# Listing each expert's first three pages first, in a two-layer graph and mixture-of-experts kernel

## The chip, the core and the metric

The kernel runs on one core of a Trainium2 chip. The metric is the device time of one execution in microseconds (us); lower is better. The engines have these names in the profile: PE is the matrix engine (its weight loads are PEld), DVE the vector engine, ACT the scalar engine, POOL the general engine, which here issues the indirect DMAs, and SP the engine whose queue issues most of the other DMAs. A suffix q (SPq, ACTq) marks what an engine's queue issues.

## What is computed

The input is 128 graphs of 64 nodes with 256 features, so 8192 tokens of 256 numbers, all in f32. There are two layers, and each is a graph convolution followed by a mixture of experts:

```
x = x + gnn0(ln(x), adj)        # adj @ h, 256->1024, rms norm, silu, 1024->256
x = x + ffn0(ln(x))             # 64 experts, the best 6 per token: sum_k score_k * (x @ lattice[e_k]), 256x256 each,
                                #   then out_w, a residual and a layer norm
x = x + gnn1(ln(x), adj)        # adj @ h @ W_rel + h @ W_root, relu
x = x + ffn1(ln(x))             # 8 experts, the best 2 per token: relu(x @ W1[e] + b1) @ W2[e] + b2, 256->512->256
```

Which experts a token goes to depends on the data. Worked out with the reference's arithmetic on its inputs, the 64 experts of ffn0 get between 278 and 1654 tokens each, 49152 in all; of the first 1024 tokens an expert gets between 45 and 201.

## The kernel before, in words

The work is done in 32 blocks of 256 tokens and in four stages, one after the other.

**Stage 1 (L550 to L760)** computes gnn0 block by block, chooses six experts per token and sends each token's row six times into a table in device memory, `r0x`, by indirect DMAs from POOL (`send`, L304, 12 a block). Each expert has chunks of rows of its own in that table. A row carries its token, the number of its place in the answer (column D) and its weight (column D+1). At the end `page_table` (L326) lists on DVE the **pages** that are to be worked off: a page is 128 rows of one expert. The order of the list is: all the full pages, expert by expert, and then the partial page of each expert. The list is made with a running sum over `num`, which holds the number of full pages of 64 experts and then 0 or 1 for their partial pages (V = 128 columns); `kind` counts how many entries of the running sum lie at or below a page's number.

**Stage 2 (L763 to L815)** works off the pages in pairs. `fetch` (L770) loads a page into `px` on SP's queue, 12 pairs ahead, into 16 buffers for each half of a pair; `flip` (L780) turns it on PE into `pxT`; `apply` (L790) multiplies it by its expert's matrix in `lat` (64 matrices, 131072 bytes a partition, resident), DVE scales the product into `py_s` (8 buffers, L806), and POOL scatters the 128 rows to their places in `r0y` (`answer` in the code) by one indirect DMA (`reply`, L311). 212 pairs (424 pages) are always done; 12 pairs more lie in a branch (`tc.If`, L814) that is taken when the list is longer than 424 pages. Any routing fits in 447 pages.

**Stage 3 (L819 to L1028), the fused pass**, does for each block: load the six answers of each of its tokens (`load3`, L848: `y<-r0y`, two DMAs a block, then `xn1` and `x1`), sum them by PE (`mixture`, L859), `out_proj`, the residual and layer norm (`layer_out_h`, `_a`, `_b`, `_c`), all of gnn1, the choice of two experts and the sending of rows into `r1x`. The pass is staggered: the list in L1007 names for each step which stage of which block comes next, and PE, DVE and ACT take their instructions in just that order (`manual_schedule`, L462). `y` has two buffers. Before the pass the second router `r1` is made (L820): constants on POOL and DVE, and two DMAs of zeros from a `filler` tile (L141 and L183 on SP's queue). Ten small loads of weights and rows come from ACT's queue (L830 to L839), and DVE adds the two gate rows (L840) before anything else of the pass.

A DMA of `y` reads `r0y`, which all replies write; so each of them waits until every reply before it in the program, those of the branch included, is done or skipped.

**Stage 4 (L1031 to L1106)** does ffn1 in pages of 256 rows, in the same manner with the router `r1`; its answers are added into the output by DMAs (L319). Its first three pages, one each of the experts 0 to 2, are known early (`look`, L146) and are listed apart.

The pools of on-chip memory are laid one behind the other: the constants, then `lat`, then stage 2's pool `wx0`, which starts with the `px` buffers. When stage 2 is over, the pools of stages 3 and 4 (`keep`, `wx1`, `c3`, `work3`) are laid from the start of `lat` on, over `lat` and part of `wx0`. A tile that lies on old memory waits for those that last used it.

Of the kernel before, what the change touches and what calls it, by code (L numbers as in the profile page):

```python
# [9 lines left out]
F32 = mybir.dt.float32  # L10
BF16 = mybir.dt.bfloat16
# [5 lines left out]
ALU = mybir.AluOpType  # L17
AX = mybir.AxisListType
PSUM = bass.MemoryType.PSUM
P = 128  # L20
# [7 lines left out]
class Ops:  # L28


    def __init__(self, nc, small, ident, eps):
        self.nc, self.small, self.ident, self.eps = nc, small, ident, eps
# [46 lines left out]
class Router:  # L79
# [12 lines left out]

    def __init__(self, tc, pool, small, dram, n, D, E, K, T, pg, S, epoch, name, total=None):
        nc = tc.nc
        self.tc, self.nc, self.pool, self.small = tc, nc, pool, small
        self.n, self.D, self.E, self.K, self.T, self.pg, self.S, self.name = n, D, E, K, T, pg, S, name
# [8 lines left out]
        self.W = D + 2  # L107
        assert T == 2 and epoch == 4 and n % self.EP == 0 and S % pg == 0 and (5 * T * P <= S or S >= n)
        assert self.pages <= 4 * P and self.spare + pg < 2 ** 24
        self.tri = pool.tile([P, P], BF16, name=name + "tri")  # L110
        self.ones = pool.tile([P, P], BF16, name=name + "ones")
        make_upper_triangular(nc, self.tri, diag=False)
        nc.gpsimd.memset(self.ones, 1.0)
        self.expert = self.iota([P, 2 * E], [[1, 2 * E]], 0, "expert")
        self.page = self.iota([P, 4], [[1, 4]], 4, "page")
        self.total, self.each = total, (1 if total is not None else K)
        self.dest = self.iota([P, T, K], [[P * self.each, T], [0 if self.each == 1 else 1, K]], self.each, "dest")
        self.base = pool.tile([P, E], F32, name=name + "base")
        nc.vector.tensor_scalar(self.base, self.expert[:, :E], float(self.pitch), None, op0=ALU.mult)
        self.zero = pool.tile([P, 2 * E], F32, name=name + "zero")  # L120
        nc.gpsimd.memset(self.zero, 0.0)
        self.map = pool.tile([P, self.J, E], F32, name=name + "map")
        nc.gpsimd.memset(self.map, 0.0)
# [22 lines left out]
    def look(self, m):  # L146
# [11 lines left out]
        v.tensor_scalar(self.firsts[:, :m], t, float(self.spare), None, op0=ALU.add)  # L158
        self.full_pages -= m

    def iota(self, shape, pattern, m, name):
        t = self.pool.tile(shape, F32, name=self.name + name)
        i = self.small.tile([P, 384], I32, name="iota", bufs=1)[:, :t.free_size()]
        if len(shape) == 3:
            i = i.rearrange("p (a b) -> p a b", b=shape[2])
        self.nc.gpsimd.iota(i, pattern=pattern, base=0, channel_multiplier=m)
        self.nc.vector.tensor_copy(t, i)
        return t
# [19 lines left out]
    def choose(self, logits):  # L188

        nc, T, E, K, n = self.nc, self.T, self.E, self.K, self.name  # L190
        top = self.small.tile([P, T, 8], F32, name=n + "top")
        idx = self.small.tile([P, T, 8], U32, name=n + "idx")
        for t in range(T):
            nc.vector.max(top[:, t, :], logits[:, t, :])
            nc.vector.max_index(idx[:, t, :], top[:, t, :], logits[:, t, :])
        which = self.small.tile([P, T, K], F32, name=n + "which")
        nc.vector.tensor_copy(which, idx[:, :, :K])
        hot = self.work.tile([P, T, K, E], BF16, name=n + "hot")
        nc.vector.tensor_tensor(hot, self.expert[:, :E].unsqueeze(1).unsqueeze(1).to_broadcast([P, T, K, E]),
                                which.unsqueeze(3).to_broadcast([P, T, K, E]), op=ALU.is_equal)  # L200
        return top, hot

# [103 lines left out]
                    in_=xs[:, t, k, :], in_offset=None)  # L306
                self.alone(i.ins, *groups)

    def reply(self, x, y):

        i = self.nc.gpsimd.indirect_dma_start(  # L311
            out=self.answer[:, :],
            out_offset=bass.IndirectOffsetOnAxis(ap=x[:, self.D:self.D + 1].bitcast(I32), axis=0),
            in_=y, in_offset=None, bounds_check=self.n * self.K - 1, oob_is_err=False)
        self.alone(i.ins, "reply")

    def add(self, i, x, y):

# [7 lines left out]
    def page_table(self, scratch):  # L326

        nc, v, E, J, n, pg = self.nc, self.nc.vector, self.E, self.J, self.name, self.pg
        V = 2 * E
        used = [0]  # L330

        def small(shape, _):
# [9 lines left out]
        if J > 1:  # L342
            t = small([E], "t")
# [2 lines left out]
            v.tensor_add(self.last, run, t)  # L346
        else:
            v.tensor_copy(self.last, run)
        num, cum = small([V], "num"), small([V], "pcum")
        full, part = num[:, :E], num[:, E:]  # L350

        v.tensor_scalar(full, cnt, 1.0 / pg, (pg - 1.0) / (2 * pg), op0=ALU.mult, op1=ALU.subtract)
        v.tensor_scalar(full, full, MAGIC, None, op0=ALU.add)
# [3 lines left out]
        if self.taken is not None:  # L357
            assert J == 1
            v.tensor_sub(full, full, self.taken)
            v.scalar_tensor_tensor(self.map[:, 0, :], self.taken, float(pg), self.map[:, 0, :],  # L360
                                   op0=ALU.mult, op1=ALU.add)
        v.tensor_tensor_scan(cum, num, self.zero, 0.0, op0=ALU.add, op1=ALU.add)
        self.total_pages = self.pool.tile([P, 1], I32, name=n + "total")
        v.tensor_copy(self.total_pages, cum[:, V - 1:V])
        le, at, ate = small([4, V], "le"), small([4, V], "pat"), small([4, E], "pate")
        kind, ispart, exp, nth, row, no = (small([4], x) for x in ("pkind", "ppart", "pexp", "pnth", "prow", "pno"))
        start = small([J, 4], "pstart")
        self.tab = self.pool.tile([P, 2, 4], I32, name=n + "tab")
        v.tensor_tensor(le, wide(cum, 1, V), wide(self.page, 2, V), op=ALU.is_le)
        v.tensor_reduce(kind, le, op=ALU.add, axis=AX.X)  # L370
        v.tensor_tensor(at, wide(self.expert, 1, V), wide(kind, 2, V), op=ALU.is_equal)
        v.tensor_mul(le, le, wide(num, 1, V))
        v.tensor_reduce(nth, le, op=ALU.add, axis=AX.X)
        v.tensor_sub(nth, self.page, nth)
        v.tensor_add(ate, at[:, :, :E], at[:, :, E:])
        v.tensor_mul(le[:, :, :E], at[:, :, E:], wide(full, 1, E))
        v.tensor_reduce(no, le[:, :, :E], op=ALU.add, axis=AX.X)
        v.tensor_add(nth, nth, no)
        for j in range(J):
            v.tensor_mul(le[:, :, :E], ate, wide(self.map[:, j, :], 1, E))  # L380
# [7 lines left out]
        v.tensor_scalar(row, row, float(self.spare), None, op0=ALU.subtract)  # L388
        v.tensor_mul(row, row, no)
        v.tensor_scalar(self.tab[:, 0, :], row, float(self.spare), None, op0=ALU.add)  # L390
        v.tensor_scalar(ispart, kind, float(E), None, op0=ALU.is_ge)
        v.scalar_tensor_tensor(exp, ispart, -float(E), kind, op0=ALU.mult, op1=ALU.add)
        v.tensor_scalar(self.tab[:, 1, :], exp, float(E - 1), None, op0=ALU.min)

    def fill_end(self, e):
# [49 lines left out]
def two_layer_gnn_moe_kernel(ctx: ExitStack, tc: tile.TileContext, a: dict, out: bass.AP):  # L445
# [7 lines left out]
    T = 2  # L453
# [4 lines left out]
    KH = H0 // P  # L458
    K0 = 6
    E1, F1, _ = a["L1_ffn_W2"].shape  # L460
    KF = F1 // P
    ctx.enter_context(tc.manual_schedule(engines={ENG.PE, ENG.DVE, ENG.Activation}))  # L462

# [60 lines left out]

    x1_dram = [dram.tile([C, D], F32, name=f"x1_{b}") for b in range(NB)]
    xn1_dram = [dram.tile([C, D], F32, name=f"xn1_{b}") for b in range(NB)]
    r0 = Router(tc, const, small, dram, N, D, E0, K0, T, P, 14 * P, 4, "r0")
    W = r0.W

    lat_pool = tc.tile_pool(name="lat", bufs=1)  # L530
    lat = lat_pool.__enter__().tile([P, E0, KD, D], F32, name="lat")
# [18 lines left out]
    with tc.tile_pool(name="c0", bufs=1) as c0, \  # L550
# [161 lines left out]
        def place(b):  # L712
            B = blocks[b]
            r0.normalize(*B["w"], B["xs"])
            r0.send(r0.places(b, B["hot"]), B["xs"])

        def load_lattice(b):
            n = free[0] // 16
# [44 lines left out]
    with tc.tile_pool(name="wx0", bufs=3) as wx, \  # L763
# [6 lines left out]
        def fetch(j):  # L770
            Q = pairs[j]
            for q in range(2):
                i = 2 * j + q
                if i % 4 == 0:
                    regs["row"] = r0.load(0, i, ENG.SP)
                if i < r0.pages:
                    Q["px", q] = px = wx.tile([P, 1, W], F32, name=f"px{q}", bufs=16)
                    r0.fetch(i, regs["row"][i % 4], px)

        def flip(j):  # L780
# [9 lines left out]
        def apply(j):  # L790
            Q = pairs[j]
            if j < E0:
                r0.fill_end(j)
            if j % 2 == 0:
                regs["e"] = r0.load(1, 2 * j, ENG.PE)
            py = py_pool.tile([P, 2, D], F32, name="py")
            y = wx.tile([P, 2, D], F32, name="py_s", bufs=8)
            n = min(2, r0.pages - 2 * j)
            for q in range(n):
                for k in range(KD):  # L800
                    nc.tensor.matmul(py[:, q, :], lhsT=Q["xT"][:, k, ts(q, P)],  # L801
                                     rhs=lat[:, ds(regs["e"][(2 * j + q) % 4], 1), k, :].rearrange("p o d -> p (o d)"),
                                     start=(k == 0), stop=(k == KD - 1))
            for q in range(n):
                px = Q["px", q]
                nc.vector.tensor_scalar(y[:, q, :], py[:, q, :], px[:, 0, D + 1:D + 2], None, op0=ALU.mult)  # L806
                r0.reply(px[:, 0, :], y[:, q, :])


        stages = ((-12, fetch), (0, apply),  # L810
                  (-2, lambda j: flip(j) if j < 4 else None), (-3, lambda j: flip(j) if j >= 4 else None))
        likely = (r0.likely_pages + 3) // 4 * 2
        staggered(likely, stages)
        with tc.If(r0.needed(2 * likely)):  # L814
            staggered(npair, stages, likely)  # L815
    lat_pool.__exit__(None, None, None)


    keep = ctx.enter_context(tc.tile_pool(name="keep", bufs=1))  # L819
    r1 = Router(tc, keep, small, dram, N, D, E1, 2, T, 2 * P, N, 4, "r1", total=out)  # L820
    fw1 = a["L1_ffn_W1b1"]
    F1W = fw1.shape[2]
    fw2 = keep.tile([P, E1, KF, D], F32, name="fw2")
# [1 line left out]
    with tc.tile_pool(name="c3", bufs=1) as c3, \  # L825
# [13 lines left out]
        gbias = load_rows(c3, "L1_ffn_bias")  # L839
        nc.vector.tensor_add(bg, bg, gbias)  # L840
        one = c3.tile([P, P], F32, name="one")
        nc.gpsimd.memset(one, 1.0)
        blocks = [dict() for _ in range(NB)]
        pg = pmix.tile([P, T, E1], F32, name="pg")
        FIRST = 3
# [2 lines left out]
        def load3(b):  # L848
            B = blocks[b]
            B["y"] = y = work.tile([P, T, K0, D], F32, name="y")  # L850
            for t in range(T):
                nc.sync.dma_start(out=y[:, t], in_=r0.answer[ts(b * T + t, P * K0), :].rearrange("(p k) d -> p k d", k=K0))
            B["xn1"] = xn1 = work.tile([P, T, D], F32, name="xn1", bufs=3)
            nc.sync.dma_start(out=xn1, in_=by_tile(xn1_dram[b]))
            B["x1"] = x1 = work.tile([P, T, D], F32, name="x1", bufs=3)
# [283 lines left out]
```

## Time and profile before

| | us |
|---|---|
| median of five runs (2135.41 to 2142.46) | 2138.4 |
| the profiled execution, its own time | 2138.43 |
| its span, first to last instruction | 2136.7 |
| busy in the span: PE / DVE / ACT / POOL | 1938.2 / 1187.1 / 1019.6 / 1166.4 |
| 424 replies (L311) on POOL: busy, mean of one | 412.5, 0.973 |
| 424 scalings (L806) on DVE: mean of one | 0.479 |
| first and last reply issued | 669.82 and 1210.30 |
| last product of stage 2 ends on PE | 1185.09 |
| first `y` load issued on SP's queue | 1214.57 |
| first sum of the fused pass on PE | 1220.67 |
| one block of the fused pass in its steady part | 11.3 |

Times in the trace count from the start of the span; the time of the execution is 1.7 us longer than its span. A line of the timeline gives start, length, engine, line, operation and how many were merged; in brackets is how long the engine sat idle before it and what ended that. A line of the waits gives the total, how often, and the longest. A line of the windows gives, for one stretch, the length, then the busy time and number of instructions of PE, PEld, DVE, ACT and POOL, the clock granted to PE (1.00 is full), the busy share of the DMA engines and what they moved in GB/s.

### The profile page before, as it was taken

How to read it: one execution, taken by the hardware profiler on the slowest of the kernel's cores; microseconds unless marked ns; L12 is line 12 of the kernel's file. 1: busy time of each engine (PE TensorE's matmuls, PEld its weight loads, DVE VectorE, ACT ScalarE, POOL GpSimd, SP SyncE). 2: the span in 40 equal slices, each digit the busy share in tenths (PEclk: the TensorE clock that was granted, in tenths of full speed). 3: DMA queues.
4: the chain of work that ended last, by engine and by line, in shares of the span. 5: the costliest groups of instructions: out<-in, count | busy, mean ns of one | idle time of the engine just before them, and what ended most of it. 6: DMA issues, size and time to landing. Idle time of an engine off the chain costs nothing. (4 is left out here: it accounts for less than half of the span.)

```text
span 2136.7 us, 37321 instructions
## 1 busy us (share of the span) xinstructions
PE 1938.2 (91%) x10564; PEld 1683.3 (79%) x10564; DVE 1187.1 (56%) x3958; ACT 1019.6 (48%) x2037; POOL 1166.4 (55%) x1146
## 2 busy tenths in 40 slices
PE   7999999999945989998888289999988999999997
PEld 6888888888835778877777278888877888888886
DVE  5889989899882333333333168888883222222221
ACT  5888788888831222222222056666653333333332
POOL 0376666666675777777777503333343344444444
PEclk9999999999967999999999699999998999999998
DMA  3244455553377887666665379888735766666665
GB/s 109 96 138 150 145 163 165 165 165 131 123 238 230 273 257 239 209 207 208 208 204 160 109 282 331 294 262 273 266 116 129 183 157 165 163 162 164 162 160 109
DMA packets 284094, 398.96 MB, mean 187 GB/s; under 512 B 56536, under 2 KB 237928, under 8 KB 283888
## 3 DMA queue, kind: packets, MB, share of 16 engines
q1 hardware_dynamic: 204032, 247.67, 39.4%
q0 software_dynamic: 64800, 136.14, 21.4%
q10 hardware_dynamic: 15056, 12.69, 1.8%
q8 instruction: 94, 1.54, 0.3%
q14 instruction: 112, 0.92, 0.2%
HBM read 223.89 MB, written 177.69 MB: 188 GB/s over the span
## 5 line engine op out<-in xcount | busy, mean ns | idle before, releaser
L304 POOL DMA_INDIRECT r0x<-xs,r0row x384 | 396.0, 1031 | 256.0 <-issue 171.7
L311 POOL DMA_INDIRECT r0y<-py_s,px x424 | 412.5, 973 | 140.8 <-DMA r0y<-py_s,px 55.2
L801 PE MATMUL py<-lat,pxT 128*128 x1696 | 410.4, 385 | 40.4 <-DVE py_s L806 22.8
L806 DVE TENSOR_SCALAR py_s<-py,px 128x256 f32<-128x256 f32 x424 | 185.7, 479 | 361.8 <-PE py L801 185.8
L801 PEld LDWEIGHTS py<-lat,pxT 128*128 128x128 f32 x1696 | 307.2, 191 | 90.5 <-ACT pxT L788 30.7
L319 POOL DMA_INDIRECT out_x<-py_s,px x138 | 214.5, 1554 | 298.7 <-DMA out_x<-py_s,px 208.9
L788 ACT COPY pxT<-pt 128x512 f32<-128x512 f32 x212 | 124.1, 586 | 429.2 <-PE pt L786 300.6
L1077 ACT ACTIVATE phid<-ph,pw 128x256 f32<-128x256 f32 x276 | 130.9, 474 | 323.1 <-issue 170.6
L1075 PE MATMUL ph<-pxT,pw 128*128 128x256 f32 x1104 | 251.5, 381 | 0.7 <-ACT pxT L1066 0.7
L1095 PE MATMUL py<-fw,phid 128*128 (+1 forms) x1104 | 249.7, 379 | 0.0
L630 PE MATMUL ph<-lat 128*128 128x256 f32 x1024 | 232.9, 386 | 11.0 <-DVE lat L652 10.4
L663 PE MATMUL ps<-lat 128*128 128x256 f32 x1024 | 237.7, 381 | 0.0
L1075 PEld LDWEIGHTS ph<-pxT,pw 128*128 128x128 f32 x1104 | 211.0, 191 | 30.1 <-ACT pxT L1066 1.1
L630 PEld LDWEIGHTS ph<-lat 128*128 128x128 f32 x1024 | 195.2, 193 | 39.4 <-DVE lat L652 10.0
L1095 PEld LDWEIGHTS py<-fw,phid 128*128 128x128 f32 x1104 | 204.5, 190 | 25.0
L663 PEld LDWEIGHTS ps<-lat 128*128 128x128 f32 x1024 | 193.2, 191 | 24.7
L304 POOL DMA_INDIRECT r1x<-xs,r1row x128 | 130.2, 1017 | 116.8 <-ACT xn3T L978 63.2
L786 PE MATMUL pt<-ident,px 128*128 128x128 f32 x848 | 128.3, 275 | 35.8 <-DMA px<-r0x 35.8
L786 PEld LDWEIGHTS pt<-ident,px 128*128 128x128 f32 x848 | 106.6, 142 | 57.7 <-issue 36.3
L1089 DVE TENSOR_SCALAR p<-p 128x2 f32<-128x2 f32 x69 | 12.0, 174 | 226.3 <-ACT p L1088 226.3
L1098 DVE TENSOR_TENSOR py_s<-py,pb 128x512 f32<-128x512 f32 x69 | 47.8, 692 | 156.0 <-PE py L1095 151.2
L866 PE MATMUL ps<-ident,y 128*128 128x128 f32 x768 | 93.7, 280 | 38.4 <-DMA r1x<-r1filler 35.6
(271 smaller groups left out, 2876.7 us busy)
## 6 DMA issues: line engine op xcount, KB each, us to landing
px<-r0x SPq DMA_DIRECT2D x424, 129.0 KB
y<-r0y SPq DMA_DIRECT2D x64, 768.0 KB
pw<-in_L_ffn_W1b SPq DMA_DIRECT2D x69, 514.0 KB
px<-r1x SPq DMA_DIRECT2D x69, 258.0 KB
x<-x SPq DMA_DIRECT2D x64, 256.0 KB
pb<-in_L_ffn_b SPq DMA_DIRECT2D x69, 128.0 KB
r0x<-r0filler ACTq DMA_DIRECT2D x64, 129.0 KB
lat<-in_x SPq DMA_DIRECT2D x32, 256.0 KB
```

What stands on the lines that cost most here:

```text
L304: i = self.nc.gpsimd.indirect_dma_start(out=self.table[:, :], out_offset=bass.IndirectOffsetOnAxis(ap=row[:, t, k:k + 1], axis=0), in_=xs[ ...
L311: i = self.nc.gpsimd.indirect_dma_start(out=self.answer[:, :], out_offset=bass.IndirectOffsetOnAxis(ap=x[:, self.D:self.D + 1].bitcast(I32 ...
L319: i, d = f"{self.name}add{i}", self.nc.gpsimd.indirect_dma_start(out=self.total[:, :], out_offset=bass.IndirectOffsetOnAxis(ap=x[:, self.D ...
L630: nc.tensor.matmul(ph[:, c, :], lhsT=w1[:, k, ts(2 * j + c, P)], rhs=B["aggT"][:, k, :], start=(k == 0), stop=(k == KD - 1))
L663: nc.tensor.matmul(B["po"][:, t, :], lhsT=B["hT"][:, c, ts(t, P)], rhs=w2[:, c, :], start=False, stop=(t == T - 1 and c == KH - 1))
L786: nc.tensor.transpose(pt[:, k, ts(q, P)], Q["px", q][:, 0, ts(k, P)], ident)
L788: nc.scalar.copy(xT[:, :, :n * P], pt[:, :, :n * P])
L801: nc.tensor.matmul(py[:, q, :], lhsT=Q["xT"][:, k, ts(q, P)], rhs=lat[:, ds(regs["e"][(2 * j + q) % 4], 1), k, :].rearrange("p o d -> p (o ...
L806: nc.vector.tensor_scalar(y[:, q, :], py[:, q, :], px[:, 0, D + 1:D + 2], None, op0=ALU.mult)
L1075: nc.tensor.matmul(ph, lhsT=w[:, k * F1 + c * P:k * F1 + (c + 1) * P], rhs=Q["xT"][:, k, :], start=(k == 0), stop=(k == KD - 1))
L1077: nc.scalar.activation(hid[:, c, :], ph, AF.Relu, bias=w[:, KD * F1 + c:KD * F1 + c + 1], scale=1.0)
L1095: nc.tensor.matmul(py[:, t, :], lhsT=Q["hid"][:, c, ts(t, P)], rhs=fw2[:, ds(e, 1), c, :].rearrange("p o d -> p (o d)"), start=(c == 0), s ...
```

## The change

1. `page_table` now lists three kinds of pages: each expert's first R full pages (R = 3 for `r0`, 1 for `r1`), then the rest of the full pages, then the partial ones. `num` has V = 3 x 64 columns, and a few small DVE operations more find expert and place from `kind`. So no page numbered 192 or higher is among an expert's first three.
2. A reply of a page numbered 192 or higher is put into a group `r0last`, and the `y` loads of blocks 0 to 3 (READY = 4) declare that they don't depend on that group. They still depend on the replies of pages 0 to 191.
3. That is sound if the rows of the first four blocks all lie in first pages. `look_back` notes after block 3 how many rows each expert has by then; if one has more than its first pages hold, `page_table` sets the page count to 447, so that the branch is taken, and a small DMA at the end of the branch waits there for all replies.
4. The router `r1` is made at the start of the kernel, next to `r0`, in the pool of constants; it takes the two constant matrices `tri` and `ones` from `r0`. To make room the `px` buffers of stage 2 go from 16 to 15 in each half.
5. The memset of `one` in stage 3 goes from POOL to DVE.

```diff
-        self.expert = self.iota([P, 2 * E], [[1, 2 * E]], 0, "expert")
...
+        if like is None:
...
+        else:
+            self.tri, self.ones = like.tri, like.ones
+        self.R = R
+        self.seen = None
+        self.expert = self.iota([P, E], [[1, E]], 0, "expert")
...
+    def look_back(self):
+
+        self.seen = self.pool.tile([P, self.E], F32, name=self.name + "seen")
+        self.nc.vector.tensor_sub(self.seen, self.run[:, 0, :], self.base)
...
-    def reply(self, x, y):
+    def reply(self, i, x, y):
...
+        self.alone(d.ins, "reply")
+        if i >= self.R * self.E:
+            self.tc.add_to_no_dep_group(self.name + "last", d.ins)
...
-        V = 2 * E
+        V = 3 * E
...
+        v.tensor_scalar(first, full, float(self.R), None, op0=ALU.min)
+        v.tensor_sub(rest, full, first)
         v.tensor_tensor_scan(cum, num, self.zero, 0.0, op0=ALU.add, op1=ALU.add)
         self.total_pages = self.pool.tile([P, 1], I32, name=n + "total")
-        v.tensor_copy(self.total_pages, cum[:, V - 1:V])
...
+            far = small([1], "far")
+            v.scalar_tensor_tensor(cnt, first, -float(pg), self.seen, op0=ALU.mult, op1=ALU.add)
+            v.tensor_reduce(far, cnt, op=ALU.max, axis=AX.X)
+            v.tensor_scalar(far, far, 0.0, float(self.pages), op0=ALU.is_gt, op1=ALU.mult)
+            v.tensor_tensor(self.total_pages, far, cum[:, V - 1:V], op=ALU.max)
...
-        v.tensor_tensor(at, wide(self.expert, 1, V), wide(kind, 2, V), op=ALU.is_equal)
+        v.tensor_scalar(two, kind, float(E), None, op0=ALU.is_ge)
+        v.tensor_scalar(three, kind, 2.0 * E, None, op0=ALU.is_ge)
+        v.scalar_tensor_tensor(exp, two, -float(E), kind, op0=ALU.mult, op1=ALU.add)
+        v.scalar_tensor_tensor(exp, three, -float(E), exp, op0=ALU.mult, op1=ALU.add)
+        v.tensor_tensor(ate, wide(self.expert, 1, E), wide(exp, 2, E), op=ALU.is_equal)
...
+        v.tensor_sub(two, two, three)
+        v.scalar_tensor_tensor(nth, two, float(self.R), nth, op0=ALU.mult, op1=ALU.add)
...
+        v.tensor_mul(no, no, three)
...
-    r0 = Router(tc, const, small, dram, N, D, E0, K0, T, P, 14 * P, 4, "r0")
+    r0 = Router(tc, const, small, dram, N, D, E0, K0, T, P, 14 * P, 4, "r0", 3)
+    r1 = Router(tc, const, small, dram, N, D, E1, 2, T, 2 * P, N, 4, "r1", 1, total=out, like=r0)
...
+            if b == READY - 1:
+                r0.look_back()
...
-                    Q["px", q] = px = wx.tile([P, 1, W], F32, name=f"px{q}", bufs=16)
+                    Q["px", q] = px = wx.tile([P, 1, W], F32, name=f"px{q}", bufs=15)
...
-                r0.reply(px[:, 0, :], y[:, q, :])
+                r0.reply(2 * j + q, px[:, 0, :], y[:, q, :])
...
+        wait = const.tile([1, 4], F32, name="wait")
         with tc.If(r0.needed(2 * likely)):
             staggered(npair, stages, likely)
+
+            nc.sync.dma_start(out=wait, in_=r0.answer[0:1, 0:4])
...
-        nc.gpsimd.memset(one, 1.0)
+        nc.vector.memset(one, 1.0)
...
-                nc.sync.dma_start(out=y[:, t], in_=r0.answer[ts(b * T + t, P * K0), :].rearrange("(p k) d -> p k d", k=K0))
+                d = nc.sync.dma_start(out=y[:, t],
+                                      in_=r0.answer[ts(b * T + t, P * K0), :].rearrange("(p k) d -> p k d", k=K0))
+                if b < READY:
+                    tc.declare_no_dep(d.ins, group="r0last", reason="in the first pages, or waited for above")
```

## The prediction

> **What bounds the kernel now.** I read the forty slices of the page first, to see where PE, the busiest engine, is not busy:
>
> ```profile
> PE   7999999999945989998888289999988999999997
> POOL 0376666666675777777777503333343344444444
> PEclk9999999999967999999999699999998999999998
> ```
>
> A slice is 53.4 us. PE has two holes: slices 11 to 13 (stages 1 to 2) and slice 23 (stages 2 to 3). In slices 13 to 22 POOL sits at 7, which is as high as it gets in stage 2: 424 replies from 669.82 to 1211.27 are 541.5 us, 1.277 us each, of which 0.97 is busy and 0.30 the gap that every reply has. So POOL bounds stage 2. From slice 24 on PE stands at 9 through stages 3 and 4. What starts stage 3 earlier therefore shortens the whole, as long as PE stays the bound behind it.
>
> Second, the timeline around slice 23 shows in what order the hole ends:
>
> ```profile
> 1183.12 1.97 PE L801 MATMUL py<-lat,pxT 128*128 x8 [0.54 <-DVE py_s L806]
> ...
> 1185.22 0.41 ACTq L492 DMA_DIRECT2D m_L_ffn_out_wT<-in_L_ffn_out_wT  x1
> ...
> 1210.30 0.97 POOL L311 DMA_INDIRECT r0y<-py_s,px  x1 [0.31 <-issue]
> 1214.09 0.20 POOL masks.py:65 MEMSET r1tri<- 128x128 bf16 x1 [2.82 <-DMA r0y<-py_s,px]
> ...
> 1214.57 0.34 SPq L852 DMA_DIRECT2D y<-r0y  x1
> 1215.36 0.40 SPq L141 DMA_DIRECT2D out_x<-r1filler  x1
> 1215.86 0.41 SPq L183 DMA_DIRECT2D r1x<-r1filler  x1
> 1216.33 0.54 SPq L852 DMA_DIRECT2D y<-r0y  x1
> ...
> 1220.67 4.77 PE L866 MATMUL ps<-ident,y 128*128 128x128 f32 x24 [35.58 <-DMA r1x<-r1filler]
> ```
>
> PE ends stage 2 at 1185.09. POOL has 21 replies left and issues the last at 1210.30; SP may issue the first y load at 1214.57, after the last has landed, and PE starts 6.1 us later. SP's own waits say the same:
>
> ```profile
> SPq L852 <- DMA r0y<-py_s,px: 38.6, 1, 38.6
> ```
>
> The reader is to see also the ACT line at 1185.22: a load into memory that `lat` held goes 0.13 us after PE's last read of `lat`, and waits for no reply. The `y` tiles lie in the same memory.
>
> Third, the windows, for what the DMA engines have to spare:
>
> ```profile
> 1185.00:1211.00 26.00, 0.09 (x1) 0.00 (x0) 3.23 (x9) 0.00 (x0) 19.90 (x21) 0.60 0.21 62
> 1211.00:1215.00 4.00, 0.00 (x0) 0.00 (x0) 0.19 (x1) 0.00 (x0) 1.18 (x8) 0.50 0.01 0
> 1215.00:1221.00 6.00, 0.33 (x2) 0.36 (x3) 0.77 (x4) 0.00 (x0) 1.33 (x7) 0.50 0.89 291
> 1221.00:1231.00 10.00, 6.65 (x33) 5.37 (x31) 1.37 (x5) 0.59 (x1) 0.00 (x0) 0.83 0.83 291
> ```
>
> While the last replies drain, the DMA engines are 0.21 busy; as the pass fills up they move 291 GB/s.
>
> **The change, part by part.**
>
> *The y loads.* Pages 0 to 191 were answered long before: reply 192 was issued near 669.8 + 192 x 1.277 = 915 us. So the first y load goes when PE frees `lat`, at about 1185.5 instead of 1214.57: 29.1 us earlier. Landing took 5.4 us, first matmul at about 1191.6.
>
> *What comes next late.* Nearly all the ramp moves with it, but not past one point. The tiles of stage 3 lie from the start of `lat`: by their sizes `fw2` 32768 bytes, `wx1` about 41250, `c3` 8900, `y` 24576, `xn1` and `x1` 12288, `accT` and `h` 4096, `x2` 4096 come to some 128000 of the 131072; the first `hn` still fits, the second and `s` lie over the first `px` buffers. Those are read by the last replies and by the branch. So `s` of block 0 (L921) must wait for the last reply, at about 1214.6. Before, it ran here:
>
> ```profile
> 1242.85 1.08 ACT L921 ACTIVATE s<-x,bn_nm,bn_rs 128x256 f32<-128x256 f32 x2
> ```
>
> That allows 1242.85 - 1214.6 = 28.2 us. By the ramp alone `s` would be ready at 1242.85 - 29.1 = 1213.8, so it waits under 1 us. The waiting instruction stands in ACT's order before the copy `accT` of block 2 and `hT` of block 0, and PE waits for those (its matmuls L877 and L938). Gain: 28.2.
>
> *Contention.* The y loads now run beside replies. Blocks 0 and 1 with their `xn` and `x` are 3.7 MB, 16.4 us before (1214.57 to 1231.0). 62 GB/s beside 291 makes them up to 3.5 us slower; that y load no longer waits for the zeros of L141 and L183 (SP's load of `xn` waited 3.8 us for L141) gives that back. The last reply's landing, 2.8 us after its issue, may rise to twice that. Bounds 0 and 5, taken 1.5, near the low end since the DMA engines were idle for four fifths of the time.
>
> DVE now works while POOL writes descriptors. Rows: in stage 1, with DVE busy, the same kind of instruction (L304) takes 1.031 us in the mean, against 0.973 in stage 2, and 1.52 at 562.91 beside DVE's L199. Some 13 replies are left when DVE is free at 1194: 13 x 0.06 = 0.8 us, at most 13 x 0.55 = 7. I take 0, as the 1.5 above covers it. The Trainium skill speaks harder against this ("SBUF — State Buffer", Who interferes with whom, and the trap above it): while DVE holds the shared port, POOL cannot write descriptors, and an indirect DMA of 620 ns took 3100. An estimate by that page, 2.5 us for each of 13 replies, would be 32 us and would eat the gain; no row of stage 1 shows such a reply.
>
> *r1 at the start.* The constants of `r1` leave the hole (POOL 1214.09 to 1215.8, hidden there) and come before the first block. DVE makes three casts in turn with three iotas on POOL; a round took 0.7 to 0.8 us for r0 (casts at 3.91, 4.69, 5.38), so 2.1, and two operations of 0.2. DVE's first statistics, at 6.02, come some 2.5 us later. In the trace DVE then waits 1.53 us for `at` until 8.71, and PE starts at 9.52. With statistics to 9.7 and ACT's 0.6, DVE's scaling (9.06) starts near 10.3: 1.2 us late. Bounds 0 and 2.5. Two DMAs of zeros, 0.4 us each, join SP's early queue, where `r0`'s was issued at 13.86 and held nothing up; I count 0, and 1 if they delay a block's load.
>
> *Page tables.* Four operations of 512 elements (0.69 us) become 768 (0.96, as L293 shows): +1.1; one of 512 goes: -0.7; about eleven small ones of 0.16 to 0.22 come: +1.9. Together +2.3 for r0. The cover:
>
> ```profile
> 646.15 0.35 DVE L393 TENSOR_SCALAR r0tab<-lat 128x4 int32<-128x4 f32 x1
> ...
> 659.92 39.94 SPq L430 DMA_DIRECT2D px<-r0x  x51
> ```
>
> POOL's sends go on to 658.0 and the first fetch waits for them until 659.92; 13 us hide it, without them it would cost 2.3. r1: +1.2; its table was ready at 1617.96 and the fetch behind it waited for sends until 1619.80; beyond that the three early pages cover it. `look_back` and the memset of `one`: under 0.3 each on DVE, 0.
>
> *Page order.* Same pages, same sizes; 412 by the reference's routing (2 full pages or more for each expert, the first 1024 tokens at most 201 rows of an expert against 256 or more), so neither the branch nor `look_back`'s alarm is taken. 0.
>
> *15 px buffers.* A fetch waits for the reply 15 pairs back instead of 16, 2.55 us later. The last fetch went at 1173.2, its flip at 1177.88, its product at 1183.12; PE's pace is set by `py_s` and so by POOL. 0, up to 2 late at PE's end, which the gate at 1214.6 absorbs.
>
> *Sum.* -28.2 + 1.5 + 1.2 = -25.5. The profiled execution took 2138.43, the median is 2138.4: 2113.
>
> **Rivals.**
>
> (a) *The ramp is held by a late row.* DVE's first operation of the pass adds the gate rows (L840). The second was issued at 1221.50 on ACT's queue, after that queue had stood behind `m_L_gnn_W_root` (issued 1220.04, when the first y had landed), and landed at 1228.99, 7.5 us later. If it now comes behind block 1's y (1185.5 + 16.4 = 1201.9), the sum is at 1209.4 and `h` at 1210.2 against 1229.81: 19.6 us less, 18 after the start's 1.2: 2120. Against: before, it came behind the first y only. 18 in 100, from 2117 to 2131 with heavier contention.
>
> (b) *Nothing happens*: another of the load's waits ends with the last reply. For: SP waits once, and the profile names only the last of several. Against: the ACT load at 1185.22. Then 2138.4 + 1.2 = 2139.6. 6 in 100.
>
> (c) *Slower: stage 2 starves with 15 buffers.* If the loop from fetch over flip, product and reply back to the fetch takes L, a pair takes the greater of 2.554 and L/15. POOL never paused with 16, so L is at most 40.9; at that, 2.727 a pair, and 212 pairs cost 36 us: 2149. It decides from L = 40.1 on. Against: fetch to product was 9.9 us, and scaling, reply and landing add about 5; the rest is queueing. 6 in 100.
>
> **How the numbers follow.** The forecast, 70 in 100, runs from 2107 (no start cost and no contention, 29.1 and some of the cold first matmuls) to 2118 (5 and 2.5). With most of (a), 2107 to 2124 holds about 8 in 10. Chances, with 0.2% (4.3 us) as what a measurement tells from no change: faster 0.88 (forecast and a), same 0.06 (b), slower 0.06 (c).
>
> **What would show it.** Right: first y load near 1186 (plus 1.2), first L866 near 1192, `s` of block 0 shortly after the last reply, then all of stage 3 and 4 shifted by one amount; replies still 1.277 apart; PE's first matmul near 10.7. Wrong: the y load still near 1214 (b); `h` waiting for L840 (a); gaps over 0.3 between replies (c), or replies above 1.5 us from 1194 on.

## The result and the profile after

The changed kernel took 2133.14 us in the median of 26 runs (2129.17 to 2139.80), the kernel before 2139.86 in 47 (2135.41 to 2147.42): a ratio of 0.9967, with a 95% interval from 0.9961 to 0.9974. That is 6.7 us less. The forecast was 25.5 less, 2113, with 2107 to 2124 as its range. The direction was right; the time lay outside the range, and the mechanism that carried the forecast did not run at all.

The slices of the changed kernel, PE and POOL:

```profile
PE   6999999999945899998999399999989999999997
POOL 1376666666676777777777504333434444444444
```

The hole in slice 23 is still there. The timeline around it (start, length, engine, line, operation, idle before) shows that its order has not changed:

```profile
1182.65 0.41 ACTq L520 DMA_DIRECT2D m_L_ffn_out_wT<-in_L_ffn_out_wT  x1
...
1207.68 0.97 POOL L321 DMA_INDIRECT r0y<-py_s,px  x1 [0.30 <-issue]
1211.90 0.82 SPq L885 DMA_DIRECT2D y<-r0y  x2
1212.27 0.61 POOL L275 TENSOR_SCALAR xs<-r1dest 128x4 int32<-128x4 f32 x3 [3.62 <-DMA r0y<-py_s,px]
...
1216.48 5.35 PE L902 MATMUL ps<-ident,y 128*128 128x128 f32 x24 [33.95 <-DMA y<-r0y]
...
1234.93 1.07 ACT L957 ACTIVATE s<-x,bn_nm,bn_rs 128x256 f32<-128x256 f32 x2
```

PE is done with stage 2 at 1182.53, ACT's load goes 0.12 us later as before, and still SP issues the first `y` load only at 1211.90, 4.22 us behind the issue of the last reply; in the kernel before it was 4.27 behind. SP's waits say it in one line:

```profile
SPq L885 <- DMA r0y<-py_s,px: 35.3, 1, 35.3
```

So the 6.7 us did not come from the load that the change was to set free. From the two traces, the lead of the changed kernel grows like this:

| point | before | after | lead |
|---|---|---|---|
| PE's first matmul | 9.52 | 10.08 | -0.6 |
| first reply issued | 669.82 | 668.19 | 1.6 |
| last reply issued | 1210.30 | 1207.68 | 2.6 |
| first `y` load | 1214.57 | 1211.90 | 2.7 |
| first sum on PE | 1220.67 | 1216.48 | 4.2 |
| `s` of block 0 | 1242.85 | 1234.93 | 7.9 |
| `s` of block 2 | 1263.62 | 1256.92 | 6.7 |

The lead at block 2 (6.7) is near what the medians differ by (6.72), but that is partly chance: each column is one execution, and the spans of these two differ by 3.3 only. In stage 4, which PE began 5.6 us earlier (1607.57 against 1613.21), the changed one lost 2.3 again.

### The profile page after: what moved, and what is told of

Its sections match the earlier page's. It is cut to its first block, busy times and chain, and to the rows that moved or that the text cites. A ratio compares the mean times of both kernels' runs of the same rounds, so it can differ in the third digit from the quotient of the medians.

```text
span 2133.4 us, 37309 instructions
## 1 busy us (share of the span) xinstructions
PE 1942.6 (91%) x10564; PEld 1684.1 (79%) x10564; DVE 1191.0 (56%) x3975; ACT 1019.0 (48%) x2037; POOL 1163.9 (55%) x1142
## 5 line engine op out<-in xcount | busy, mean ns | idle before, releaser
L819 ACT COPY pxT<-pt 128x512 f32<-128x512 f32 x212 | 123.9, 585 | 427.5 <-PE pt L817 303.8
```

Source lines behind the costliest of these rows:

```text
L819: nc.scalar.copy(xT[:, :, :n * P], pt[:, :, :n * P])
```

## The experiments

Two questions: what ties the first `y` load, and what gave the 6.7 us. Theory A: the memory ties it. The first use of a pool's memory waits for everything that used any memory under that pool, not under the tile alone. `work3`, in which `y` lies, reaches from `lat` over the `px` buffers. Theory B: the table `r0y` still ties it, the declaration does not reach it. Theories C and D concern the gain: the declaration (C) or the order of the pages (D).

Beside e1 to e5 and f1 to f4 the kernel before itself took 2465 to 2467 us instead of 2139. The replies came 1.53 us apart, and only 5 to 8 were issued behind the end of PE's last product (20 in the profile of before). So little was to be had from draining them, and the times of these runs hardly tell the variants apart; they are read by the moments in their traces. Two measures serve: the first `y` load less the issue of the last reply, and `s` of block 0 less the first `y` load, called the ramp below.

**e1, e2, e3, e4: one tie at a time.** e1 gives `y` and what goes with it a pool of their own that ends inside the memory of `lat`:

```diff
             tc.tile_pool(name="c3", bufs=1) as c3, \
+            tc.tile_pool(name="first3", bufs=2) as first, \
             tc.tile_pool(name="work3", bufs=2) as work, \
...
-            B["y"] = y = work.tile([P, T, K0, D], F32, name="y")
+            B["y"] = y = first.tile([P, T, K0, D], F32, name="y")
```

and so for `xn1`, `x1`, `accT`, `h` and `x2`. e2 takes the declaration out of the changed kernel, e4 out of e1:

```diff
-                if b < READY:
-                    tc.declare_no_dep(d.ins, group="r0last", reason="in the first pages, or waited for above")
```

e3 is the kernel before with `r1` made at the start, and with 15 `px` buffers to make room for it:

```diff
+    r1 = Router(tc, const, small, dram, N, D, E1, 2, T, 2 * P, N, 4, "r1", total=out)
...
-                    Q["px", q] = px = wx.tile([P, 1, W], F32, name=f"px{q}", bufs=16)
+                    Q["px", q] = px = wx.tile([P, 1, W], F32, name=f"px{q}", bufs=15)
...
-    r1 = Router(tc, keep, small, dram, N, D, E1, 2, T, 2 * P, N, 4, "r1", total=out)
```

> The changed kernel with one edit: the tiles y, xn1, x1, accT, h and x2 lie in a pool of their own, first3, which ends inside the memory of lat; the rest stays in work3. Theory A (pools): the first use of a pool's memory waits for everything that used any memory under that pool; work3 reaches from lat into the px buffers, so its first y load waits for the last replies whatever is declared of r0y. Then y goes when PE is done with lat, near 1184 instead of 1211.9, and s of block 0 is held by the last reply: after has it at 1234.9, 23 us behind the last landing; less 1.5 for contention, the time is 21 us under the changed kernel, near 2112. Theory B (the table): the load still depends on the replies through r0y, the declaration does not reach it; then y stays at 1211.9 and the time at 2133.

> The changed kernel without the declaration on the y loads (they depend on all replies again). Theory A: the declaration removes nothing that the pool does not ask for anyway; the same as the changed kernel, 2133, 0.9967 of before. Theory C (the 6.7 us are what the declaration brings, through the loads of blocks 1 to 3): back to before, 2140.

> The kernel before with one part of the change: r1 is made at the start, in the pool of constants with its own two matrices, and px has 15 buffers. Page order and y loads as before. Theory A: the measured gain is this part's. The zeros leave SP's queue between the y loads (first sum 4.6 us behind the first y load instead of 6.1) and the gate rows are issued some 5 us earlier; near 2134, 0.997. Theory D (the gain is the order of the pages, by a stage 2 that starts and ends sooner): 2140 to 2141.

> As e1_split, with the pool first3, but without the declaration on the y loads. Theory A: both ties have to go; here the table's holds y until the last reply has landed, so 2131 to 2134, as the changed kernel. If the split alone gave the gain (the table was never a tie in effect), 2112.

Measured against the kernel before: e1 0.9981 (0.9945 to 1.0016), e2 0.9988 (0.9946 to 1.0029), e3 0.9995 (0.9949 to 1.0041), e4 0.9990 (0.9955 to 1.0025). As times these are misses: no interval leaves 1 out. e1, e2 and e3 were run again in another session, and e1 in a third:

> The same kernel as e1_split (y, xn1, x1, accT, h and x2 in a pool of their own inside the memory of lat), asked again, because in e1_split's session every kernel, the one before too, took some 330 us longer and PE set the pace of stage 2, so that no replies were left to drain. Theory A (pools): y goes near 1184, s of block 0 is held by the last reply, 21 us under the changed kernel, near 2112, 0.987 of before. Theory B (the table still ties the load): 2133, 0.9967.

> The same kernel as e2_depend (the changed kernel without the declaration), asked again for the same reason. Theory A: the same as the changed kernel, 2133, 0.9967. Theory C (the declaration brings the 6.7 us): 2140, 1.000.

> The same kernel as e3_r1early (the kernel before with r1 made at the start and 15 px buffers), asked again for the same reason. Theory A: the measured gain is this part's, near 2134, 0.997. Theory D (the gain is the order of the pages): 2140 to 2141, 1.000.

> The same kernel as e1_split and e1b_split (y, xn1, x1, accT, h and x2 in a pool of their own inside the memory of lat), a third time, in a later session. If the kernel before takes 2138 again and 21 replies are left behind PE's last product: theory A near 2112 (0.987), theory B 2133 (0.9967). If it takes 2466 again with some 8 replies left: at most the 8 replies' 10 us are to be had, 0.996 to 1.000 either way, and only the moment of the first y load tells the theories apart.

Again 0.9975 (0.9927 to 1.0023), 1.0003 (0.9948 to 1.0057), 1.0023 (0.9987 to 1.0058) and 0.9991 (0.9932 to 1.0050). The moments are clear, and each repeats:

| kernel | pool apart | declaration | `y` load less last reply | `s` less `y` load |
|---|---|---|---|---|
| before | no | no | +4.3 | 28.3 |
| e3, e3b (before, r1 early) | no | no | +4.2, +4.2 | 22.9, 22.7 |
| after | no | yes | +4.2 | 23.0 |
| e2, e2b | no | no | +4.2, +4.2 | 22.9, 22.8 |
| e4 | yes | no | +4.0 | 22.9 |
| e1, e1b, e1c | yes | yes | -2.95, -4.4, -5.5 | 29.7, 29.8, 29.6 |

Only with both ties gone does the load pass the last reply. The declaration alone does nothing (after and e2 are alike), so C falls, and the pool alone does nothing (e4): theory A. B falls with e1, where the declaration does reach the load. One rival is left, that the wait is by tile after all and `y` itself is laid over `px`. The addresses in the built kernels rule it out: in the changed kernel `lat` ends at byte 170240 of a partition, where `px` begins, and the two buffers of `y` take 122080 to 146656, in e1 the same bytes. And the shorter ramp, 23 us instead of 28, comes with r1's move and its 15 buffers (e3), without the new order of pages: D falls for that part.

e1's last column holds a new fact: where the load goes early, the ramp behind it is longer again, 30 us. What it waits for, in e1b, is block 1:

```profile
1503.35 0.82 SPq L886 DMA_DIRECT2D y<-r0y  x2
...
1513.54 0.94 SPq L886 DMA_DIRECT2D y<-r0y  x2
...
1520.10 0.69 DVE L920 TENSOR_TENSOR h<-po,xn 128x512 f32<-128x512 f32 x1
...
1520.89 4.90 PE L903 MATMUL ps<-ident,y 128*128 128x128 f32 x24 [4.61 <-DMA y<-r0y]
...
1525.88 0.59 ACT L906 COPY accT<-ps 128x512 f32<-128x512 f32 x1 [11.64 <-PE ps L903]
...
1533.12 1.08 ACT L958 ACTIVATE s<-x,bn_nm,bn_rs 128x256 f32<-128x256 f32 x2
```

In ACT's order the copy `accT` of block 1 stands ahead of block 0's last steps, and `s` of block 0 runs 7.24 us behind it here, in the kernel before, in the changed one and in e6 (7.23). The copy waits for block 1's sums on PE, and these for block 1's `y`, which SP issued 10.2 us behind block 0's (6.7 in the changed kernel). Between them SP had stood for a row that ACT had loaded:

```profile
SPq L891 <- DMA r_L_ffn_ln_g<-in_L_ffn_ln_g: 8.0, 1, 8.0
```

The add of the two gate rows was late as well: it ran at 1519.83 on DVE, and `h` behind it at 1520.10, where `po` had been finished at 1516.3. But `h`'s statistics were ready at 1522.0 and ACT took them up at 1527.78, behind the copy, so the rows did not hold `s`.

**e5: everything of the pass in the memory of `lat`.** The pools are only laid in another order:

```diff
+    c3 = ctx.enter_context(tc.tile_pool(name="c3", bufs=1))
+    work = ctx.enter_context(tc.tile_pool(name="work3", bufs=2))
     keep = ctx.enter_context(tc.tile_pool(name="keep", bufs=1))
...
-    with tc.tile_pool(name="c3", bufs=1) as c3, \
-            tc.tile_pool(name="work3", bufs=2) as work, \
-            tc.tile_pool(name="ps3", bufs=3, space=PSUM) as psum, \
+    with tc.tile_pool(name="ps3", bufs=3, space=PSUM) as psum, \
```

> The changed kernel with the pools of stage 3 laid first: c3 and work3 before keep and wx1, so that all tiles of the fused pass lie in the memory of lat (130400 of 170240) and fw2 and wx1 come behind. No other edit. Theory A: y goes near 1184 and nothing of the pass is held by the last replies up to block 4's load, which falls due later than they land; the whole ramp moves by 28, less 1.5 for contention: 2106 to 2108, 0.985, some 4 us under e1b_split. If s of block 0 was no gate in e1b_split, the two are alike. If DVE's work beside the replies holds POOL up, the replies come apart by more than 1.3 us and the time is over 2115.

> The same kernel as e5_all_in_lat (the pools c3 and work3 first, so that the whole fused pass lies in the memory of lat), asked again: in that session every kernel took some 330 us longer, with PE and ACT setting the pace of stage 2 and 6 replies left behind PE's last product, where the profile of before has 21. With 21 left: y near 1184, and 2106 to 2108 (0.985) by theory A; 2133 (0.9967) if something else still holds the ramp.

Against the kernel before it took 1.0018 (0.9971 to 1.0066) and 0.9987 (0.9960 to 1.0013); the first `y` load went 1.95 and 4.1 us ahead of the last reply, and the ramp was 30.2 in both. Nothing was settled on the time.

**f1 to f4: a bound that was not restored.** Two memsets on POOL behind each reply were to make POOL the bound:

```diff
         self.alone(d.ins, "reply")
+        for _ in range(2):
+            self.nc.gpsimd.memset(self.small.tile([P, 384], I32, name="iota", bufs=1), 0)
```

> The changed kernel with two memsets of 128x384 on POOL behind every reply, so that POOL bounds stage 2 again, as in the profile of before: 1.277 us a reply become about 2.1, stage 2 about 890 us, and some 21 replies (44 us) are left behind PE's last product. It is the base for the next three runs. By theory A (pools) the first y load goes when the last reply has landed; by theory C (the declaration works) some 40 us ahead of it.

> As f1_after_slowpool, with y, xn1, x1, accT, h and x2 in the pool first3 inside the memory of lat. Theory A: y goes within 8 us of PE's last product, some 40 us ahead of the last reply; DVE is free for the pass when 13 replies are left (27 us); s of block 0 waits for the last reply. In the run of the changed kernel s came 23 us after the first y load, so 21 to 24 us less than f1. Theory B (the table ties the load): no difference.

> As f1_after_slowpool, with c3 and work3 laid first, so that no tile of the pass lies over px. Theory A with a gate at s: s of block 0 is free too, and what holds next is the y load of block 4, which must wait for the last reply; it was issued 21 us after the first y load, and its sum came 15 us behind its issue: 30 to 36 us less than f1, 8 to 12 less than f2. If s was no gate: the same as f2.

> The kernel before with the same two memsets behind every reply. Between f1 and this one lies the change alone with POOL as the bound: theory A (the gain is r1's move, 1.5 us at the y load and some 4 us at the gate rows): f1 5 to 7 us less. Theory D (the order of the pages shortens stage 2): f1 less by what its last reply is earlier.

The memsets wait for no data, and POOL's order is not written by hand here: all 848 ran between 7.4 and 801.6, ahead of the replies. Again only 5 to 7 replies were left; f1 took 2595.0, f2 2587.0, f3 2589.5, f4 2587.1, with ranges that overlap (f1 2589 to 2604, f2 2581 to 2598). The moments agree with the table: f1 +5.2 and f4 +4.3, f2 -4.0 and f3 -5.4; the ramp 23.0 in f1 and 29.7 in f4, 30.4 and 29.4 in f2 and f3.

**g1 to g3: POOL as the bound.** The filler now reads the product, so it can't run ahead:

```diff
         self.alone(d.ins, "reply")
+        for _ in range(2):
+            self.nc.gpsimd.tensor_copy(self.small.tile([P, 384], F32, name="iota", bufs=1)[:, :self.D], y)
```

g1 is the changed kernel with it, g2 is e1 with it, and g3 is e5 with it and one more edit, the two gate rows first on ACT's queue:

```diff
+        bg = load_rows(c3, "L1_ffn_bg")
+        gbias = load_rows(c3, "L1_ffn_bias")
         out_wT = load_matrix(c3, "L0_ffn_out_wT")
```

> The changed kernel with two copies of py_s on POOL behind every reply; they read the scaled product, so they cannot run ahead of it, as the memsets of f1 did (all 848 ran before the replies). POOL bounds stage 2: about 2.1 us a reply, stage 2 near 890 us, some 21 replies (44 us) left behind PE's last product. Theory A (pools): the first y load only when the last reply has landed, s of block 0 some 23 us later. Base for the next two.

> As g1_after_poolbound, with y, xn1, x1, accT, h and x2 in the pool first3 inside the memory of lat. Theory A: y goes within 8 us of PE's last product, near 40 us ahead of the last reply. DVE is free when some 13 replies are left (27 us), so h would allow s about 13 us ahead of the last reply; s lies over px and waits for its landing. From 26 us behind the last reply to 3 behind it: 23 us less than g1. If the tie is elsewhere: no difference.

> As g1_after_poolbound, with c3 and work3 laid first (no tile of the pass over px) and the two gate rows first on ACT's queue. s is free of the last reply; block 4's y load, which waits for it, is some 6 us late behind its slack: 30 to 36 us less than g1, 8 to 12 less than g2. If s was no gate in g2, or the rows no matter: the same as g2.

Beside these three the kernel before took 2139 us, and 2140 beside e6. Against it g1 took 1.1709 (1.1687 to 1.1731), g2 1.1614 (1.1591 to 1.1637), g3 1.1546 (1.1524 to 1.1568): in the medians 2503.2, 2484.0 and 2468.6, so 19.2 and 34.7 us less than g1, where 23 and 30 to 36 were expected; the step from g2 to g3, 15.4, was expected at 8 to 12. Replies came 2.155 us apart, and 22 were left behind PE's last product. g1, the last product and the first load:

```profile
1535.14 1.97 PE L834 MATMUL py<-lat,pxT 128*128 x8 [0.53 <-DVE py_s L839]
...
1588.72 0.82 SPq L887 DMA_DIRECT2D y<-r0y  x2
```

g2, the same, and ACT's first work in the memory of `work3`:

```profile
1536.17 1.29 SPq L888 DMA_DIRECT2D y<-r0y  x2
1541.07 2.79 PE L905 MATMUL ps<-ident,y 128*128 128x128 f32 x12 [5.01 <-DMA y<-r0y]
...
1587.91 1.09 ACT L956 ACTIVATE hn<-x,bn_nm,bn_rs 128x256 f32<-128x256 f32 x2 [20.04 <-DMA r0y<-py_s,px]
...
1588.91 1.07 ACT L960 ACTIVATE s<-x,bn_nm,bn_rs 128x256 f32<-128x256 f32 x2
```

The load goes 0.1 us behind PE's last product and 46 us ahead of the last reply (1582.2). Then ACT stands 20 us at `hn` until the last reply has landed. The first `hn` still lies in the memory of `lat` (bytes 167136 to 169184 of the built kernel); it waits because it is the first of a pool that reaches over `px`. This is theory A once more, on another tile.

g3, where no pool of the pass reaches over `px`:

```profile
1571.25 1.08 ACT L959 ACTIVATE s<-x,bn_nm,bn_rs 128x256 f32<-128x256 f32 x2
...
1588.72 0.81 SPq L887 DMA_DIRECT2D y<-r0y  x2
```

`s` of block 0 is 17.7 us earlier than in g2 and 40.2 earlier than in g1. Now it is the `y` load at 1588.72 that waits for the last reply, and PE waits 1.5 us for it (1593.17). The step from g2 to g3 is two edits, but the rows gave nothing here: their add ran 19.8 us behind the first `y` load in g2 and 19.6 in g3.

**e6: the cure without the filler.** g3 without the copies on POOL: all of the computation is as in the changed kernel, the pools are in another order, and the gate rows are first.

> The changed kernel with c3 and work3 laid first (no tile of the fused pass over px) and the two gate rows first on ACT's queue; nothing added on POOL, every part of the computation as in the changed kernel. Theory A, where the kernel before takes 2139: y near 1184 and its sum near 1190, DVE free at 1192.6 (last scaling in the changed kernel), so h near 1198 and s of block 0 near 1209 instead of 1234.9; block 4's y load falls due near 1207 and waits until 1212, which its slack of 12 us covers. 24 to 27 us less than the changed kernel: 2106 to 2110, 0.985 to 0.987 of before. If DVE's work beside the replies holds POOL up: 2115 and more.

2107.94 us in the median of five (2106.49 to 2108.15), 0.9847 of the kernel before (0.9834 to 0.9861) and so clear of the changed kernel's 0.9967 (0.9961 to 0.9974), too; between the medians, of two sessions, lie 25.2 us, where 24 to 27 were expected. It is faster than both kernels, and it falls inside the range that was forecast for the changed kernel. Its timeline:

```profile
1182.86 1.59 SPq L885 DMA_DIRECT2D y<-r0y  x2
...
1189.63 5.17 PE L902 MATMUL ps<-ident,y 128*128 128x128 f32 x24 [6.90 <-DMA y<-r0y]
...
1207.61 0.97 POOL L321 DMA_INDIRECT r0y<-py_s,px  x1 [0.30 <-DVE bn_sd L931]
...
1212.19 1.08 ACT L957 ACTIVATE s<-x,bn_nm,bn_rs 128x256 f32<-128x256 f32 x2
...
1214.95 0.81 SPq L885 DMA_DIRECT2D y<-r0y  x2
1215.07 0.96 POOL L275 TENSOR_SCALAR xs<-r1dest 128x4 int32<-128x4 f32 x3 [6.49 <-DMA r0y<-py_s,px]
```

`y` goes 0.13 us behind PE's last product and 24.7 us ahead of the last reply; `s` of block 0 is 22.7 us earlier than in the changed kernel, `s` of block 2 (1231.28) 25.6. That the rows had a part in it is not shown: with them first the ramp is 29.3, without 30.2 (e5), and in both it ends 7.2 us behind block 1's copy `accT`. The windows of the changed kernel and then of e6, from 1186 to 1211 (length, busy time and number of PE, PEld, DVE, ACT, POOL, clock, DMA share, GB/s):

```profile
1186.00:1211.00 25.00, 0.00 (x0) 0.00 (x0) 2.63 (x6) 0.00 (x0) 17.46 (x18) 0.54 0.18 52
```

```profile
1186.00:1211.00 25.00, 16.67 (x90) 14.28 (x90) 8.41 (x26) 3.23 (x6) 17.40 (x18) 0.80 1.01 356
```

The hole is filled: PE works 16.7 of its 25 us, the DMA engines are full, and POOL's 18 replies are not touched. In the slices of e6 the hole at 23 is gone:

```profile
PE   6999999999964999999999799999989999999997
```

## Why the prediction was wrong, step by step

**The `y` loads (-28.2): the step that failed.** "A load into memory that `lat` held goes 0.13 us after PE's last read of `lat`, and waits for no reply. The `y` tiles lie in the same memory." Both sentences hold, and what was concluded from them, that `y` would go as early, does not. The ACT load's tile is in `c3`, a pool that lies wholly in `lat`; `y` is in `work3`, which begins in `lat` and ends over `px`. The wait is by pool. The description of the kernel puts it on the tile ("a tile that lies on old memory waits"); it is the whole pool that waits. Measured: the declaration alone moved the load by nothing (+4.2 in after and e2), so the term was 0 instead of 28.2. The tile sizes of the prediction were the right list; the sum had to be made by pool. Rival (b), that another of the load's waits ends with the last reply, is what happened. It had 6 in 100, on the strength of the one line that seemed to speak against it.

**The gate at `s`: right in kind, a tile too late.** g2 shows it, at `hn`, because it is by pool as well. The prediction gave the early load 28.2 up to that gate; e6, where the load is early and no such gate stands, has `s` of block 2 25.6 earlier than the changed kernel, and 32.3 earlier than the kernel before, of which the changed kernel had 6.7 already. So what an early load would bring was sized about right; it is the wait that was wrong.

**r1 out of the hole: costed at nothing, worth 5.3 us at `s` of block 0.** "Hidden there" was wrong. The two DMAs of zeros stood on SP's queue between the halves of block 0's `y`: load to first sum took 6.1 us before, 4.6 after. They also stood ahead of block 1's `y`, on which the ramp hangs, and moved 0.5 MB. In the kernel before block 1's sums and ACT's copy of them:

```profile
1231.02 4.51 PE L866 MATMUL ps<-ident,y 128*128 128x128 f32 x24 [2.86 <-DMA y<-r0y]
...
1235.61 0.59 ACT L869 COPY accT<-ps 128x512 f32<-128x512 f32 x1 [9.50 <-PE ps L866]
```

and in the changed kernel the second half of the sums and the copy:

```profile
1226.07 1.53 PE L902 MATMUL ps<-ident,y 128*128 128x128 f32 x12 [0.20 <-DMA y<-r0y]
...
1227.69 0.58 ACT L905 COPY accT<-ps 128x512 f32<-128x512 f32 x1 [5.18 <-PE ps L902]
```

The copy runs 21.04 us behind the first `y` load before and 15.79 after, and the 5.25 between them are all of the difference between the ramps (28.28 and 23.03). The gate rows of rival (a) were late before as well (the add at 1228.99, `h` at 1229.81; after 1221.52 and 1224.64), but `h`'s statistics were ready at 1231.7, and ACT took them up at 1237.51, behind the copy: (a) was not what held the ramp. e3 shows that the move, with 15 buffers, shortens the ramp from 28.3 to 22.9; 1.2 of the lead is given back by block 2. As a time of its own the move is not shown (e3 0.9995, e3b 1.0023).

**The first 2.7 us** are there at the first `y` load already: the first reply is 1.6 us earlier (e6 has it at 668.0, too), and the replies are 1.2754 apart instead of 1.2777. g1, g2 and g3, which are like the changed kernel up to there, have their first reply at 671.2, 669.5 and 671.2, so the 1.6 is no more than single executions differ by. Whether order, buffers or the new start did any of it, no run tells. It stays open. 2.7 + 5.3 - 1.2 is 6.8, beside 6.7 measured, but the first term is not secured.

**Contention (+1.5): too small, and of another kind.** In e6, where the loads do run beside the replies, the ramp from `y` to `s` takes 29.3 us instead of 23.0, so 6.3; 2.9 of it is made good by block 2. Replies are still 1.278 apart with DVE busy for a third of the time, and none is longer than 1.00 us. By the estimate from the Trainium skill that the prediction weighed against the change ("SBUF — State Buffer", Who interferes with whom) they would have been 2.5 us longer. That page's price is for a `tensor_copy` on DVE, while DVE's work here was two-input operations, scalings and statistics, so these replies do not test the rule itself. The last landing did stretch: POOL waited 6.5 us behind the last reply, 3.6 in the changed kernel. And SP's queue in e6 stood for a weight that ACT had loaded:

```profile
SPq L890 <- DMA m_L_ffn_out_wT<-in_L_ffn_out_wT: 8.3, 1, 8.3
```

Its load of `xn` waits for the landing of an ACT load that it has nothing to do with, and block 1's `y`, behind it, goes 11.4 us after block 0's instead of 6.7. The prediction's 3.7 MB for blocks 0 and 1 are too few as well: with four DMAs of `y` of 768 KB and four of 256 KB they are 4.2 MB.

**The small terms.** r1 at the start: 0.56 measured at PE's first matmul, 1.2 expected, inside its bounds. r0's page table is ready 1.9 us later (648.42 against 646.50), 2.3 expected, and POOL's sends hid it. 15 buffers: the replies came no further apart (1.2754 us); rival (c) did not come.

## What to carry to other kernels

Before a load is freed from data it need not wait for, list everything else that ties it, and take memory by the unit in which waits are kept, here the whole pool: one tile that reaches over old buffers ties all its neighbours. Where a neighbour is seen to go early, ask whether it is in the same pool. And a queue's small errands (zeros, weights) in the hole before a pass are not hidden there: the pass's first loads stand behind them. Before a late operand is blamed, look which wait ends last: here `h` was late and cost nothing, because the next engine was busy waiting for block 1.

## What the runs showed that was not expected

- A load on SP's queue stands for the landing of a load of ACT's queue though no data joins them: 8.3 us for `m_L_ffn_out_wT` in e6, 8.0 for `r_L_ffn_ln_g` in e1b, 8.2 in the second run of e5. When the two groups of loads are brought together in time, block 1's `y` goes later, and the ramp is longer (29 to 30 us instead of 23 in e1, e5, f2, f3 and e6). What ties the queues the traces do not say.
- Where the kernel before took 2465 us, ACT, DVE and PE stood for several microseconds at a time with no releaser on this core that the trace could name; in e1b ACT's copies (L819) waited so 34 times for 163.8 us, at most 10.7. The replies came 1.53 us apart in place of 1.28. The cause stays open.
- With the DMA engines full (1.01 of their time, 356 GB/s) for 25 us, replies still took 0.97 us each.
